# Four graph layers on one core: a chunk's first vector passes ordered behind layer 0's scaling, and half the node transfers of three groups begun on POOL's queue

## The chip, the cores and the metric

The kernel runs on one core of a Trainium2 chip. The metric is the device time of one execution in microseconds (us); lower is better. Each row of a table that comes from a trace is one execution; the medians are of several. Ratios are computed as the mean time of one kernel's runs over the mean of the other's of the same rounds, so they are not quite the ratios of the medians that are quoted. "Chunk" is 8 of the 128 graphs; "unit" is one of the 16 pieces into which layer 0's work is cut (0 to 2 of group 1, 3 and 4 of group 2, 5 and 6 of group 3, 7 and 8 of group 4, 9 to 15 of group 0).

## The reference

Four graph layers on 128 graphs of 64 nodes with 256 features, each followed by a residual and a layer norm. Only the parts that the argument touches:

```python
# layer 0: five groups of nodes, two normalised graph convolutions each
for g, idx in enumerate(GROUPS):            # 25, 9, 7, 6 and 6 of the first 25 nodes
    A = adj[:, idx][:, :, idx] + eye
    deg = A.sum(-1)
    norm_adj = deg**-0.5 * A * deg**-0.5
    h   = relu(norm_adj @ (x[:, idx] @ W1[g]) + b1[g])
    fused[:, idx] += w[g] * relu(norm_adj @ (h @ W2[g]) + b2[g])
x = layernorm(x + fused)
# layer 1: adj + eye, degree-normalised;   layer 2: a polynomial of adj / rowsum(adj)
# layer 3: five GRU steps on A = (adj != 0), the bulk of the matmuls
```

## The kernel before

TensorE's (PE's) instructions are issued in program order. The other engines' orders come from a scheduler at build time: it places an instruction where it expects its inputs to be there, and may move it well ahead of its place in the program. `tc.issue_after(ins)` adds an order behind `ins` on the same engine; it adds no wait.

The first passes over a chunk (`mid`) and the loads of layer 0:

```python
def mid(c):
    a64 = adjs.pop(c)                                    # the chunk's adjacency, loaded on SyncE's queue
    Ab = keep.tile([128, NP, 128], F32, name="Ab", bufs=1)
    nc.vector.tensor_mul(Ab..., a64..., pair...)         # first pass
    A01 = ...                                            # Ab != 0
    nc.vector.tensor_reduce(rsum, a64, AX.X, ALU.add)    # second reader of the load
    ...                                                  # rdeg, rinv, d1 (a power on POOL), dg, An
    nc.scalar.activation(poly, dg, AF.Identity, scale=cw[:, 2:3])
    yield                                                # [cut: transposes, products, layers 1 and 2]

def load0(i, after=None):
    qx = nc.gpsimd if i < 3 else nc.sync
    # [cut: tiles and the list of runs]
    for rows, t, b, f in runs:
        qa[t % len(qa)].dma_start(a[rows, t, :w], adj[b, f, 0:w])
    with tc.issue_after(after.ins) if after else nullcontext():
        for rows, t, b, f in runs:
            qx.dma_start(xg[rows, t, :], x[b, f, :])

def prep(i):                                             # on VectorE, with one power on POOL:
    # ae = a + eye; deg; d0 = deg**-0.5; ae *= d0; A0 = blocks of ae
    # PE transposes A0 into PSUM; then the "scaling of transposes":
    for v in scale:
        with tc.high_priority():
            evictions.append(nc.vector.tensor_mul(*v))   # AT

for i in range(-2, NU + 1):
    # [cut] add(i-1), aggregate(i+1), support(i), finish(i-1); then a stage of mid;
    # prep(i+2), hidden(i+1); at i == g0 (9): load_adj(0), load_adj(1)
```

## Time and profile before

| | before |
|---|---|
| device time, median of 3 | 2215.43 us (2214.81 to 2216.5) |
| span of the profiled execution | 2214.5 us |
| PE busy | 2180.2 us, 98% |
| PE idle | 34.3 us, of which 17.6 in one place at 106 to 125 us |
| first product of layer 3 | at 349.14 us |

Read it from PE: an engine that is busy 98% of the time leaves only its gaps to win, and what it does slowly; one gap is half of all gaps. The traced execution took 2216.3 us and is none of the three. The lines that show it are in the prediction below.

### The profile page before, as it was taken

How to read it: one execution, taken by the hardware profiler on the slowest of the kernel's cores; microseconds unless marked ns; L12 is line 12 of the kernel's file. 1: busy time of each engine (PE TensorE's matmuls, PEld its weight loads, DVE VectorE, ACT ScalarE, POOL GpSimd, SP SyncE). 2: the span in 40 equal slices, each digit the busy share in tenths (PEclk: the TensorE clock that was granted, in tenths of full speed). 3: DMA queues.
4: the chain of work that ended last, by engine and by line, in shares of the span. 5: the costliest groups of instructions: out<-in, count | busy, mean ns of one | idle time of the engine just before them, and what ended most of it. 6: DMA issues, size and time to landing. Idle time of an engine off the chain costs nothing.

```text
span 2214.5 us, 30166 instructions
## 1 busy us (share of the span) xinstructions
PE 2180.2 (98%) x11542; PEld 1911.4 (86%) x11542; DVE 1372.5 (62%) x3088; ACT 1003.1 (45%) x1853; POOL 571.0 (26%) x621
## 2 busy tenths in 40 slices
PE   9979999999999999999999999999999999999997
PEld 6657888888889889888889898888898898888886
DVE  3344666665766666666766676657666666566546
ACT  3233334445545454445454454455454544455453
POOL 3211122222222223223222222222222232232221
PEclk9989999999999999999999999999999999999999
DMA  5531210000100000000100010001000000000000
GB/s 166 178 109 55 58 46 4 1 3 1 41 1 4 1 20 22 3 1 7 35 1 3 1 41 1 3 1 41 1 1 1 20 10 1 1 10 11 1 1 20
DMA packets 54172, 51.12 MB, mean 23 GB/s; under 512 B 20878, under 2 KB 49036, under 8 KB 54028
## 3 DMA queue, kind: packets, MB, share of 16 engines
q1 hardware_dynamic: 49664, 43.96, 6.5%
q0 software_dynamic: 1936, 4.83, 0.8%
q8 instruction: 91, 1.49, 0.3%
q10 hardware_dynamic: 2428, 0.41, 0.1%
q14 instruction: 53, 0.43, 0.1%
HBM read 32.40 MB, written 16.78 MB: 22 GB/s over the span
## 4 chain that ended last, share of the span: by engine, by line
PE 94%; SPq 2%; DVE 1%; issue 1%; DMA 1%; ACT 0%; POOL 0%; POOLq 0%; DVEq 0%; ACTq 0%
PE parz L731 25%; PE pdrz L731 12%; PE pan L731 12%; PE pa L210 9%; PE pbrz L731 6%; PE pdn L731 6%; PE pT L772 4%; PE ps L442 4%; PE ph L426 3%; PE pbn L731 3%; PE pd L286 2%; PE pd L307 2%; SPq L362 1%; PE pa L411 1%; PE po L464 1%
## 5 line engine op out<-in xcount | busy, mean ns | idle before, releaser
L748 ACT COPY c<-parz 128x512 f32<-128x512 f32 x240 | 140.6, 586 | 322.4 <-PE parz L731 321.7
L731 PE MATMUL parz<-Th,WHH 128*128 128x256 f32 x960 | 286.0, 379 | 0.3 <-ACT c L748 0.3
L731 PE MATMUL parz<-Ta,V 128*128 128x256 f32 x960 | 285.8, 379 | 0.0
L711 POOL TENSOR_TENSOR Th<-hn 128x512 f32<-128x512 f32 x64 | 81.4, 1272 | 778.3 <-DVE hn L834 602.8
L831 ACT ACTIVATE NI<-NI,bih 128x512 f32<-128x512 f32 (+1 forms) x162 | 115.9, 715 | 206.0 <-DVE NI L826 205.8
L748 ACT COPY c<-pan 128x512 f32<-128x512 f32 x237 | 139.0, 586 | 150.1 <-PE pan L731 150.1
L731 PEld LDWEIGHTS parz<-Ta,V 128*128 128x128 f32 x960 | 182.5, 190 | 24.7
L731 PEld LDWEIGHTS parz<-Th,WHH 128*128 128x128 f32 x960 | 176.5, 191 | 21.1 <-ACT c L748 0.7
L803 ACT ACTIVATE RZ<-RZ,brz 128x512 f32<-128x512 f32 x160 | 116.0, 726 | 138.9 <-DVE RZ L760 138.9
L711 POOL TENSOR_TENSOR Ta<-agg 128x512 f32<-128x512 f32 x80 | 102.0, 1275 | 260.0 <-ACT agg L214 260.0
L760 DVE TENSOR_TENSOR RZ<-pdrz,c 128x512 f32<-128x512 f32 x80 | 55.0, 688 | 173.2 <-PE pdrz L731 173.2
L139 POOL TENSOR_TENSOR rs<-ve,mhalf 128x4 f32<-128x4 f32 (+3 forms) x67 | 68.9, 1029 | 298.3 <-DVE ve L137 234.4
L731 PE MATMUL pan<-Ta,V 128*128 128x256 f32 x474 | 141.3, 380 | 0.0
L731 PE MATMUL pan<-Th,WHH 128*128 128x256 f32 x474 | 141.1, 379 | 0.0
L754 DVE TENSOR_TENSOR NI<-pbn,c 128x512 f32<-128x512 f32 x79 | 54.6, 692 | 127.8 <-PE pbn L731 110.2
L210 PEld LDWEIGHTS pa<-A,h 128*128 128x128 f32 x1024 | 124.4, 192 | 3.3
L210 PE MATMUL pa<-A,h 128*128 128x128 f32 x1024 | 124.6, 275 | 0.0
L750 DVE TENSOR_TENSOR NI<-pdn,c 128x512 f32<-128x512 f32 x79 | 54.5, 689 | 112.7 <-ACT c L748 112.7
L832 DVE TENSOR_TENSOR RZ<-hn,NI 128x512 f32<-128x512 f32 (+1 forms) x129 | 87.8, 680 | 49.5 <-ACT NI L831 49.5
L834 DVE TENSOR_TENSOR hn<-RZ,NI 128x512 f32<-128x512 f32 (+1 forms) x161 | 109.8, 682 | 1.8
L833 DVE TENSOR_TENSOR RZ<-RZ 128x512 f32<-128x512 f32 (+1 forms) x161 | 109.5, 680 | 1.8
L442 PE MATMUL ps<-W,hg 128*125 128x256 f32 (+5 forms) x464 | 103.6, 380 | 0.3 <-ACT v L313 0.3
(220 smaller groups left out, 5077.0 us busy)
## 6 DMA issues: line engine op xcount, KB each, us to landing
out_dram<-xt SPq DMA_DIRECT2D x32, 256.0 KB
W<-in_w_dram SPq DMA_DIRECT2D x10, 512.0 KB
xt<-xb SPq DMA_DIRECT2D x32, 156.0 KB
xo<-in_x_dram SPq DMA_DIRECT2D x9, 512.0 KB
xb<-xo SPq DMA_DIRECT2D x9, 512.0 KB
xt<-xa SPq DMA_DIRECT2D x32, 100.0 KB
xg<-in_x_dram SPq DMA_DIRECT2D x25, 125.0 KB
xa<-xg SPq DMA_DIRECT2D x25, 125.0 KB
```

Source lines behind the costliest of these rows:

```text
L139: nc.gpsimd.tensor_tensor(rs[:r, :n], ve[:r, :n], mhalf[:r, :n], ALU.pow)
L210: nc.tensor.matmul(p[:, q * 128 : (q + 1) * 128], src[:, q, k * 128 : (k + 1) * 128], m[:, q, :], start=True, stop=True)
L442: nc.tensor.matmul(p[: u.rows[t], t - v, :], hg[:, e, u.off[t] : u.off[t] + u.rows[t]], W2[:, u.g, e, :], start=e == 0, stop=e == 3,)
L711: nc.gpsimd.tensor_sub(t[:, 0:2, :], a[:, :, H:], a[:, 0, :].rearrange("p (s n) -> p s n", s=2))
L731: nc.tensor.matmul(bank[:, g, :], w[:, q, i - 1, :], rhs, start=i in (1, 2, 5) and g == 0 and m == 0, stop=m == len(side) - 1, skip_group_ ...
L748: nc.scalar.copy(c, self.a)
L772: nc.tensor.transpose(p[:, q * 128 : (q + 1) * 128], src(q, k), ident)
L803: nc.scalar.activation(RZ[:, q, 0, :], RZ[:, q, 0, :], AF.Sigmoid, bias=b[0])
L831: nc.scalar.activation(n, n, AF.Tanh, bias=bih[:, 4 + j : 5 + j])
L832: e.tensor_sub(d, self.hT[:, j, f], n)
L833: e.tensor_mul(d, d, z)
L834: e.tensor_add(self.hn[:, j, f], d, n)
```

## The change

Its intent: the chunk's first passes shall not stand in front of layer 0's preparations, and SyncE's queue, which begins one transfer after another, shall be rid of part of its load.

```diff
-        nc.vector.tensor_mul(
-            Ab..., a64..., pair...)
+        with tc.issue_after(evictions[-1].ins):
+            nc.vector.tensor_mul(
+                Ab..., a64..., pair...)
         A01 = keep.tile([128, NP, 128], F32, name="A01", bufs=4)
         nc.vector.tensor_scalar(A01, Ab, 0.0, None, op0=ALU.not_equal)
-        nc.vector.tensor_reduce(rsum, a64, AX.X, ALU.add)
+        with tc.issue_after(evictions[-1].ins):
+            nc.vector.tensor_reduce(rsum, a64, AX.X, ALU.add)
@@ load0
-            qx = nc.gpsimd if i < 3 else nc.sync
+            qx = [nc.gpsimd] if i < 3 else [nc.sync, nc.gpsimd] if u.g > 1 else [nc.sync]
@@
-                    qx.dma_start(xg[rows, t, :], x[b, f, :])
+                    qx[t % len(qx)].dma_start(xg[rows, t, :], x[b, f, :])
```

(The operands of the first pass are shortened here.) "Part one" is the order, "part two" the queue.

More of the change, by code (lines that the diff above doesn't have):

```diff
@@ L225, in mid @@
         Ab = keep.tile([128, NP, 128], F32, name="Ab", bufs=1)
-        nc.vector.tensor_mul(
-            Ab.rearrange("p q (b m) -> p q b m", b=2),
-            a64[:, :, None, :].to_broadcast([128, NP, 2, N]),
-            pair[:, None, :, :].to_broadcast([128, NP, 2, N]),
-        )
+        with tc.issue_after(evictions[-1].ins):
+            nc.vector.tensor_mul(
+                Ab.rearrange("p q (b m) -> p q b m", b=2),
+                a64[:, :, None, :].to_broadcast([128, NP, 2, N]),
+                pair[:, None, :, :].to_broadcast([128, NP, 2, N]),
+            )
         A01 = keep.tile([128, NP, 128], F32, name="A01", bufs=4)
```

## The prediction

> **What bounds the kernel now.** I read first the page's busy shares and the chain that ended last, then the list of whom TensorE (PE) waited for, then the engines' timelines around the longest of those waits.
>
> ```profile
> PE 2180.2 (98%) x11542; PEld 1911.4 (86%) x11542; DVE 1372.5 (62%) x3088; ACT 1003.1 (45%) x1853; POOL 571.0 (26%) x621
> PE 94%; SPq 2%; DVE 1%; issue 1%; DMA 1%; ACT 0%; POOL 0%; POOLq 0%; DVEq 0%; ACTq 0%
> ```
>
> PE is busy 98% of the span and is 94% of the chain. The time can therefore only fall by what PE stands idle, or by what it does slowly; the span of 2214.5 less 2180.2 busy leaves 34.3 us. The chain has 2% on SyncE's queue (SPq) and 1% on a DMA: one place where PE is not the bound. The waits of PE say which:
>
> ```profile
> PE pT L397 <- DVE A L389: 15.1, 1, 15.1
> PE pT L860 <- DVE hn L834: 4.1, 3, 1.6
> PE ph L426 <- ACT ag L416: 2.5, 1, 2.5
> PE pf L560 <- ACT w L700: 1.9, 1, 1.9
> ```
>
> One wait of 15.1 us is almost half of the idle time, and the 2.5 us one follows directly after it. The timeline of VectorE (DVE) shows what DVE was doing (columns: start, duration, engine, line, operation; in brackets the idle time before it and what ended it):
>
> ```profile
> 93.63 0.16 DVE L121 TENSOR_TENSOR d0s<-deg,d0z 126x4 f32<-126x4 f32 x1
> 119.25 0.69 DVE L226 TENSOR_TENSOR Ab<-a,pair 128x512 f32<-128x512 f32 x1 [25.46 <-DMA a<-in_adj_dram]
> 119.86 0.15 DVE L125 SCALAR_TENSOR_TENSOR d0o<-deg,d0r 126x4 f32<-126x4 f32 x1
> 120.26 0.17 DVE L386 TENSOR_TENSOR ae<-ae,d0o 126x24 f32<-126x24 f32 x1
> 120.68 0.75 DVE L389 TENSOR_TENSOR A<-ae,block 126x252 f32<-126x252 f32 x2
> ```
>
> The reader is to see that chunk 0's first pass, Ab (line 226), stands in DVE's order in the middle of the preparation of layer 0's unit 7 (0 to 15, four units before the one where the program calls the chunk). It waits 25.5 us for the chunk's adjacency. The three steps behind it need only unit 7's own data, and PE needs their result. Why the adjacency is late is in SyncE's timeline: its load is issued behind eight node transfers.
>
> ```profile
> 104.39 7.57 SPq L362 DMA_DIRECT2D xg<-in_x_dram  x8
> 112.00 2.35 SPq L191 DMA_DIRECT2D a<-in_adj_dram  x2
> ```
>
> What PE lost is in its own timeline, with an undisturbed pair of the same shapes from two units later:
>
> ```profile
> 99.71 6.64 PE L442 MATMUL ps<-W,hg 128*126 128x256 f32 x30
> 121.48 1.10 PE L397 MATMUL pT<-ident,A 126*126 126x126 f32 x4 [15.13 <-DVE A L389]
> 125.07 5.31 PE L426 MATMUL ph<-ag,W 128*128 128x264 f32 x16 [2.48 <-ACT ag L416]
> 130.22 1.95 PE L464 MATMUL po<-AT,s 126*128 126x126 f32 x16
> ...
> 157.67 3.73 PE L426 MATMUL ph<-ag,W 128*128 128x264 f32 x16
> 161.24 1.95 PE L464 MATMUL po<-AT,s 126*128 126x126 f32 x16
> ```
>
> The same 16 matmuls take 5.31 us after the stall and 3.73 us later: the stall also costs clock. The table of stretches shows it (us, busy by engine, granted clock, DMA share, GB/s):
>
> ```profile
> 121.00:125.00 4.00, 1.10 (x4) 0.71 (x4) 3.10 (x19) 1.58 (x4) 1.39 (x1) 0.50 0.63 169
> 125.00:131.00 6.00, 5.93 (x24) 4.99 (x24) 3.95 (x18) 3.19 (x8) 2.43 (x2) 0.74 0.30 110
> 131.00:140.00 9.00, 9.00 (x55) 6.87 (x54) 5.78 (x33) 3.65 (x6) 2.24 (x3) 1.00 0.40 119
> ```
>
> **What the Trainium skill says.** (1) "TensorE: Matmul & The Clock Gate", the paragraph on engine queue depths: ACT and DVE are strict FIFO. The trace agrees: d0o needed a power that POOL had started at 93.93 us and that took 1.01 us, yet it ran at 119.86, right behind Ab. (2) Same page, Part 1 on the clock gate: an idle window of about 3.4 us drops the array to half clock, and about as long a busy stretch restores it. The trace agrees: 0.50 after the stall, 0.74, then 1.00. (3) "DMA: Bandwidth & Descriptors", "Issuing engines are not separate DMA queues": issuing from several engines saves only sequencer time. So the second part can buy issue time on SyncE, not bandwidth. No number of this trace tests it directly. (4) "SBUF — State Buffer", "SBUF: two separate sides": a DMA begun on POOL needs POOL to write descriptors, which some DVE operations lock out. In this trace POOL's node transfers land in 2.6 to 4.7 us beside a working DVE; I see no lockout.
>
> **Part one: Ab and the row sum behind the scaling of transposes.** The edge fixes an order on DVE and adds no wait. Chunk 0's first stage is called at unit index 10, when the last scaling of transposes traced is unit 11's, which ran at 188.68 us; Ab now comes behind it, some 69 us after its data arrived (119.25). So Ab waits for nothing, and unit 7's preparation runs on: power until 94.94, d0o, the 0.17 us scaling and two products of together 0.75 us, done at about 96.5 by the durations above. PE reaches those transposes at 106.34, so about 10 us of slack. The 15.1 us wait goes.
> The 2.5 us wait goes with it: ScalarE's copy ag stood in order behind the chunk's poly (line 248, run at 123.42 after 26.03 us of idling for DVE's dg), which also moves back.
> The gain, from the chain in order of time: PE's products end at 106.34 and the po group begins at 130.38, 24.04 us. Undisturbed, four transposes (157.40 to 157.84, 0.44 us) and sixteen matmuls (3.56 us) take 4.00. The gain is 24.04 - 4.00 = **20.0 us**: 15.1 + 2.5 of waiting and the rest slow clock.
> What it moves: Ab 0.6, A01 0.3, rsum 0.3, An 0.6, dg 0.6 and eight small ones of 0.08 each, some 3 us of DVE, from the stall to behind 188.68 on the old clock. Unit 12's preparation there ended at 199.04 and PE came for it at 206.54: 7.5 us of slack takes the 3 us. Chunk 0's own transposes come at 213.85. For chunk 1 the pass goes behind unit 14's scaling (253.43), with its transposes at 267.0; DVE is busy 13.5 of 20 us there, so it fits with less room. Later chunks had their passes long after layer 0, so the edge binds nothing; row sums of chunks 2 and 3 that ran early move to the end of layer 0, where DVE is fuller. I allow 0.5 us for both.
>
> **Part two: half the node transfers of groups 2 to 4 on POOL.** Units 3, 4, 5 and 7 give 4 of 8 issues each, units 6 and 8 (three tiles) 2 of 6: 20 issues. SyncE sheds 20 x 0.736 us = 14.7 us of issuing; POOL gains 20 x 0.62 = 12.4 us by the median of its ten node issues. Once part one is in, the adjacency has some 70 us to spare and PE waits for no other load, so 14.7 us of earlier issue is worth nothing directly. The cost: POOL is on the preparation's path through the power of 1.01 us. Four issues in front of a power hold it 2.5 us. Most preparations end 5 to 9 us before PE wants them, but unit 1's ends at 16.6 for 18.7, and unit 4's at 54.2 for 54.8. Units 3 to 5 also have unused buffers, so their transfers may be begun early, about 11 to 18 us, where the DMA engines were busiest (0.88 in the first 20 us) and where DVE waited 3.65 us for unit 1's adjacency. I allow 1 us on average for new waits here.
>
> **Sum.** 2215.43 - 20.0 + 0.5 + 1.0 = 2196.9, say 2197 us, 0.8% less.
>
> **The rivals.** (a) A wait takes the place of the old one: behind DVE's Ab stand the passes over other nodes (xo), loads of 512 KB that took 10.4 us once, and with PE 20 us earlier DVE may come to one too soon. For: the SyncE queue is in the chain. Against: DVE's waits show no xo load, and SyncE gets 14.7 us lighter. It would leave 5 to 10 us of the gain away: 2202 to 2207. (b) POOL becomes the trouble: powers of units 1 and 4 held by issues, or early loads slowed. For: slacks of 2.1 and 0.6 us. Against: POOL is busy only 26%. It would cost 3 to 8 us, with a cold clock where a stall passes some microseconds: 2198 to 2204. (c) Part two alone is what helps, the adjacency then coming 15 us earlier at about 104 us, and part one nothing more. It would give the same time within the stall's 20 us, so it can't be told by the total. (d) Something in the long third layer shifts: PE has 98% there and no wait of note, so nothing I see.
>
> **Range and chances.** All 34.3 us of idle gone would be 2181, and 2% is 44 us (below 2171): faster by 2% is out of reach of this change. Slower by 2% would need new stalls of 64 us against the gain. The range goes from the gain with nothing given back and 2 us of luck (2193) to rival (a) at its worst (2207).
>
> **What would show it right or wrong.** Right: the 15.1 and 2.5 us waits are gone from PE's list, Ab stands behind unit 11's scaling with no DMA wait, the granted clock is 1.00 from 20 to 335 us, PE's busy time falls by some 2 us, and layer 3 starts 18 to 20 us sooner. Part one is wrong if another DVE wait stops PE between 95 and 330 us; part two if a wait of PE before 60 us goes back to a POOL power or a load. The prediction fails if the gain is under 8 us, or over 22.

## The result, and the profile after

The changed kernel takes 2197.85 us (median of 4, 2197.42 to 2199.79) beside 2215.97 us of the kernel before: ratio 0.9919, 95% interval 0.9902 to 0.9937. That is 18 us or 0.8% less. The prediction was 2197 us.

The lines of the page and of PE's waits that answer to those of before:

```profile
PE 2178.3 (99%) x11542; PEld 1908.3 (87%) x11542; DVE 1372.5 (62%) x3088; ACT 1003.1 (46%) x1853; POOL 583.1 (27%) x641
```

```profile
PE pT L862 <- DVE hn L836: 4.3, 3, 1.8
PE pf L562 <- ACT w L702: 1.9, 1, 1.9
PE pw L536 <- DVE zero L533: 1.5, 1, 1.5
```

The waits of 15.1 and 2.5 us are gone and none has come in their place. PE's busy time is 1.9 us less for the same 11542 matmuls. The timeline of VectorE (DVE) around unit 7's preparation, and where Ab is now (start, duration, then engine, line, operation, output and input; idle time before in brackets; "..." marks lines left out):

```profile
94.75 0.16 DVE L121 TENSOR_TENSOR d0s<-deg,d0z 126x4 f32<-126x4 f32 x1
96.09 0.16 DVE L125 SCALAR_TENSOR_TENSOR d0o<-deg,d0r 126x4 f32<-126x4 f32 x1 [1.19 <-POOL d0r L123]
...
96.51 0.75 DVE L391 TENSOR_TENSOR A<-ae,block 126x252 f32<-126x252 f32 x2
...
107.93 0.68 DVE L403 TENSOR_TENSOR AT<-pT,d0o 126x504 f32<-126x504 f32 x1 [7.78 <-PE pT L399]
...
169.74 0.68 DVE L403 TENSOR_TENSOR AT<-pT,d0o 125x500 f32<-125x500 f32 x1 [8.08 <-PE pT L399]
...
175.23 0.66 DVE L227 TENSOR_TENSOR Ab<-a,pair 128x512 f32<-128x512 f32 x1
175.88 0.41 DVE L236 TENSOR_REDUCE rsum<-a 128x4 f32<-128x256 f32 x1
```

Between the steps d0s and d0o there is now only the power on POOL (1.19 us of idle time in place of 25.5 us). The products A are done at 97.3 us and PE takes them at 107.29. Ab runs at 175 us behind unit 11's scaling, with no wait for its load. The timeline of PE, and the granted clock in the stretch that held the stall (columns as in the prediction):

```profile
107.29 0.60 PE L399 MATMUL pT<-ident,A 126*126 126x126 f32 x4
107.72 3.73 PE L428 MATMUL ph<-ag,W 128*128 128x264 f32 x16
111.29 1.95 PE L466 MATMUL po<-AT,s 126*128 126x126 f32 x16
...
330.28 0.59 PE L733 MATMUL parz<-hT,WHH 128*128 128x256 f32 x2
```

```profile
100.00:121.00 21.00, 21.00 (x115) 17.44 (x115) 7.47 (x38) 7.11 (x13) 2.24 (x3) 1.00 0.47 149
```

The sixteen matmuls take 3.73 us in place of 5.31, and PE is busy for all of these 21 us, with a granted clock of 1.00. SyncE begins the adjacency at 93.42 us in place of 112.00, 18.6 us sooner:

```profile
82.50 10.87 SPq L364 DMA_DIRECT2D xg<-in_x_dram  x8
93.42 2.35 SPq L191 DMA_DIRECT2D a<-in_adj_dram  x2
```

**Where the time went, in three stretches.** The profiled executions are split at the first transposes of unit 0 and at the first product of layer 3.

| stretch | before | after | difference |
|---|---|---|---|
| start to first transposes | 8.58 | 9.65 | +1.07 |
| first transposes to layer 3 | 340.56 | 320.63 | -19.93 |
| layer 3 to the end | 1865.36 | 1865.92 | +0.56 |
| span | 2214.5 | 2196.2 | -18.3 |

The gain is all in the middle stretch, and it is nearly the 20.04 us worked out. For the first stretch the cause is not shown. PE's warm-up products begin at 1.49 us in both and take 7.26 us before, 8.32 us after; three traced executions of the changed kernel took 8.32, 7.06 and 7.79 us for them, so one program varies by as much. Yet over all traces the first transposes lie at 9.07 to 9.76 us in the nine with both edges of part one and at 8.55 to 8.86 us in the four without. In two of the nine PE waited there behind a load (0.66 us in after_again, for a preparation whose adjacency came late; 0.96 us in all_pool, for the identity). Whether the change has a part in it stays open. The third stretch hides a full microsecond, which the experiments trace: from ScalarE's last scaling to the end it is 3.82 us before and 4.83 us after.

### The profile page after: what moved, and what is told of

Its sections match the earlier page's. It is cut to its first block, busy times and chain, and to the rows that moved or that the text cites.

```text
span 2196.2 us, 30203 instructions
## 1 busy us (share of the span) xinstructions
PE 2178.3 (99%) x11542; PEld 1908.3 (87%) x11542; DVE 1372.5 (62%) x3088; ACT 1003.1 (46%) x1853; POOL 583.1 (27%) x641
## 3 DMA queue, kind: packets, MB, share of 16 engines
q8 instruction: 91, 1.49, 0.3%
## 4 chain that ended last, share of the span: by engine, by line
PE 96%; DVE 2%; issue 1%; POOL 1%; ACT 0%; DMA 0%; POOLq 0%; ACTq 0%; DVEq 0%
PE parz L733 25%; PE pdrz L733 12%; PE pan L733 12%; PE pa L210 9%; PE pbrz L733 6%; PE pdn L733 6%; PE ps L444 4%; PE ph L428 4%; PE pT L774 4%; PE pbn L733 3%; PE pd L288 3%; PE pd L309 2%; PE pa L413 1%; PE po L466 1%; PE pp L278 1%
```

## The experiments

All outputs are right. In the table, "middle" is the stretch from the first transposes to layer 3 and "end" the time from the start of ScalarE's last scaling to the end, both from the profiled execution; "POOL" is the number of transfers begun on POOL's queue in all.

| run | median us | ratio to before | middle | end | POOL |
|---|---|---|---|---|---|
| before | 2213.48 to 2214.83 | 1 | 340.56 | 3.82 | 31 |
| after_again | 2197.91 | 0.9926 (0.9914 to 0.9938) | 320.66 | 4.84 | 51 |
| order_only | 2196.83 | 0.9921 (0.9909 to 0.9933) | 320.59 | 3.81 | 31 |
| pool_only | 2210.94 | 0.9985 (0.9971 to 0.9999) | 336.59 | 4.85 | 51 |
| ab_edge_only | 2220.26 | 1.0025 (1.001 to 1.0039) | 342.02 | 3.84 | 31 |
| early_adj | 2211.38 | 0.9984 (0.9971 to 0.9998) | 332.06 | 3.79 | 31 |
| all_pool | 2208.68 | 0.9975 (0.9961 to 0.9988) | 328.67 | 6.82 | 75 |
| order_stores4 | 2197.59 | 0.9927 (0.9915 to 0.994) | 323.23 | 4.01 | 31 |
| order_stores2 | 2196.76 | 0.9923 (0.991 to 0.9937) | 320.60 | 3.71 | 31 |
| after_fewer | 2197.06 | 0.9923 (0.9911 to 0.9936) | 320.10 | 3.81 | 39 |
| order_again | 2197.97 | 0.9925 (0.9912 to 0.9939) | 320.59 | 3.86 | 31 |
| after_third | 2198.32 | 0.993 (0.9917 to 0.9942) | 320.59 | 4.80 | 51 |

The profiled execution of order_stores4 is the slowest of its five (2199.57); its middle is 2.6 us longer than that of its sister order_stores2, with a granted clock of 0.95 from 300 to 333 us. Executions as slow come in other builds too (2199.46 of after_again, 2198.34 of order_only, 2200.05 and 2199.75 of after_third); what sets them off was not followed.

The builds that keep a stall vary more: the kernel before took 2210.51 to 2219.22 us, part one alone 2196.42 to 2198.34. A "middle" with a stall in it is therefore good to a few microseconds only. The traced execution of the kernel before is some 2 us above its later medians, that of pool_only is the slowest of its four, those of ab_edge_only and early_adj the fastest of theirs.

### after_again: the changed kernel as the measure

No edit.

> The changed kernel unaltered, as the measure for the others on the same chip. Both theories: 2197 to 2200 us, ratio to the kernel before 0.991 to 0.993. The start of its first transposes should differ between executions by up to about 1 us (9.65 us in the profile of the changed kernel, 8.58 before), if that difference is the phase of the clock gate and not the change.

The time is as expected: 2197.91 us. The first transposes came at 9.21 us, with the same program as the one of 9.65. That does not show the clock as the reason: here the warm-up products were done sooner (7.06 us in place of 8.32), and PE then waited 0.66 us for a preparation.

### order_only: part one alone

```diff
-            qx = [nc.gpsimd] if i < 3 else [nc.sync, nc.gpsimd] if u.g > 1 else [nc.sync]
+            qx = [nc.gpsimd] if i < 3 else [nc.sync]
```

> Part one alone (Ab and row sum behind the scaling of transposes), all node transfers of groups 2 to 4 on SyncE again. My theory, that the order on VectorE is the whole gain: within 1.5 us of the changed kernel, 2196 to 2199 us; the chunk's adjacency is still issued late, at about 112 us, and nobody waits for it; no TensorE wait over 2 us before 330 us. Rival, that the transfers on POOL are needed for the gain (SyncE's queue would become the bound once the stall is gone): over 2203 us, with a wait of VectorE or TensorE for a load.

Measured: 2196.83 us, the middle stretch 320.59 us. The whole gain is there without part two. SyncE's timeline and VectorE's show why the late load doesn't matter:

```profile
112.44 2.20 SPq L191 DMA_DIRECT2D a<-in_adj_dram  x2
```

```profile
174.64 0.66 DVE L227 TENSOR_TENSOR Ab<-a,pair 128x512 f32<-128x512 f32 x1
```

The load is as late as in the kernel before (112.00), and its first reader stands 62 us behind its issue. The rival, that SyncE would become the bound, falls.

### pool_only: part two alone

The two lines of `load0` on the kernel before, without the edges on Ab and the row sum.

> Part two alone. Rival (c) of the prediction, that an adjacency issued 15 us earlier ends the stall by itself: 2197 to 2201 us. My theory, that the order is what counts: in this build Ab stands in VectorE's order one unit earlier still, in the preparation of unit 6, whose transposes TensorE wants at about 89 us; the load is issued at about 93 and lands at about 100, so VectorE waits from 78 to 100 and TensorE 10 to 15 us, and the time is 2208 to 2216 us: the 15 us won on SyncE are eaten by the earlier place.

Measured: 2210.94 us, in the range of the order theory and far from the rival's. The load was indeed begun 22.6 us sooner (89.40 us), but the scheduler had moved Ab forward with it, from unit 7's preparation into unit 6's. VectorE's waits and PE's:

```profile
DVE Ab L226 <- DMA a<-in_adj_dram: 18.0, 1, 18.0
```

```profile
PE pT L397 <- DVE A L389: 9.6, 2, 8.8
PE ph L426 <- ACT ag L416: 2.8, 2, 2.4
```

VectorE waits 18.0 us in place of 25.5, PE 12.4 in place of 17.6, and the middle stretch gains 4.0 us of 20 (by the medians the kernel gains 2.5 us). An earlier load under a scheduler that follows it is worth much less than its 22.6 us.

### ab_edge_only: half of part one

```diff
         with tc.issue_after(evictions[-1].ins):
             nc.vector.tensor_mul(Ab..., a64..., pair...)
-        with tc.issue_after(evictions[-1].ins):
-            nc.vector.tensor_reduce(rsum, a64, AX.X, ALU.add)
+        nc.vector.tensor_reduce(rsum, a64, AX.X, ALU.add)
```

(without part two.)

> Part one halved: only Ab is held back, the row sum of the same load is free, and no transfers on POOL. My theory, that any pass on the late load stops VectorE: the row sum stands in unit 7's preparation where Ab stood, waits some 25 us for the adjacency, TensorE waits 13 to 16 us, and the time is 2212 to 2217 us. Rival, that Ab alone made the wait and the row sum came only after it: 2197 to 2200 us.

Measured: 2220.26 us, 0.25% slower than the kernel before and above my range. The row sum took Ab's place, as expected. But PE was stopped by another way than I wrote:

```profile
115.82 0.42 DVE L235 TENSOR_REDUCE rsum<-a 128x4 f32<-128x256 f32 x1 [21.79 <-DMA a<-in_adj_dram]
```

```profile
118.55 0.72 ACT L249 ACTIVATE poly<-dg,cw 128x512 f32<-128x512 f32 x1 [23.54 <-DVE dg L245]
```

```profile
PE ps L443 <- ACT hg L431: 18.9, 1, 18.9
```

ScalarE's poly, three steps behind the row sum, stood in ScalarE's order between two of layer 0's activations (hg). ScalarE kept its order too: it idled 23.5 us in front of poly with hg behind it, and PE waited 18.9 us for hg. So holding back one reader freed nothing here while another reader of the same load was left. The edge on the row sum alone was not run.

### early_adj: neither part, only an earlier call of the load

```diff
-            elif i == g0:
-                for c in (0, 1):
-                    load_adj(c)
             elif i == 4:
+                for c in (0, 1):
+                    load_adj(c)
```

> Neither part of the change; only the call that loads the adjacency of chunks 0 and 1 stands five units earlier in the program. My theory, that the stall is the time from when TensorE wants a preparation to when the load in front of it lands, whatever the load's own place: VectorE's order follows the load forward, Ab stands in unit 6's preparation (wanted by TensorE at about 88 us), the load is issued at about 83 and lands at 90 to 92, so TensorE waits 3 to 8 us plus some 2 us for ScalarE's copy and slow clock: 2202 to 2209 us, between the kernel before and the changed one. Rival, that an earlier load simply mends it: 2195 to 2199 us. Rival, that the load's place is without effect because the order adapts fully: 2212 to 2217 us.

Measured: the profiled execution 2207.63 us, the other three 2211.15 to 2211.88; median 2211.38, 2 us above my range, so the sizing missed. The load was begun at 80.39 us and Ab's wait came as worked out, but a second wait was not in my account (the trace is of the fastest execution, so it need not hold all of the median's loss):

```profile
85.84 0.69 DVE L226 TENSOR_TENSOR Ab<-a,pair 128x512 f32<-128x512 f32 x1 [10.89 <-DMA a<-in_adj_dram]
118.09 0.42 DVE L234 TENSOR_REDUCE rsum<-a 128x4 f32<-128x256 f32 x1 [12.48 <-DMA a<-in_adj_dram]
```

The second is chunk 2's row sum, which the scheduler moved into unit 7's preparation once its buffer was free sooner; PE waited 3.3 us there for the scaling of transposes. Together with pool_only this settles that moving the load is no cure: the reader moves with it.

### all_pool: part two at more than twice the dose

```diff
-            qx = [nc.gpsimd] if i < 3 else [nc.sync, nc.gpsimd] if u.g > 1 else [nc.sync]
+            qx = [nc.gpsimd] if i < 3 or u.g > 1 else [nc.sync]
```

> The changed kernel with all node transfers of groups 2 to 4 on POOL, twice the dose of part two (44 issues in place of 20). My theory, that POOL has room: the stretch from the first transposes of layer 0 to layer 3's first products stays at 320.3 to 321.5 us (20 issues: 320.6), and the time within 1.5 us of the changed kernel. Rival (b) of the prediction, that issues hold POOL's powers: waits of TensorE for a preparation before 60 us, 2199 to 2204 us. The end after ScalarE's last scaling was 3.8 us in the builds without part two and 4.8 in those with it: if transfers on POOL cause that, it grows to about 6; if the position of the last store among the eight semaphores that the queues use in turn causes it (the same here as in the changed kernel), it stays at 4.8.

Measured: 2208.68 us, above even the range that the rival gave (2199 to 2204). My theory that POOL has room is wrong at this dose, and rival (b) of the prediction holds. In POOL's timeline fourteen transfers stand in front of the power that unit 2's preparation needs, and the first of them waits for POOL's own earlier transfers to land; VectorE and PE wait behind:

```profile
24.76 8.07 POOL L364 DMA_DIRECT2D xg<-in_x_dram  x14 [3.52 <-DMA xg<-in_x_dram]
32.70 1.25 POOL L123 TENSOR_TENSOR d0r<-d0s,mhalf 126x1 f32<-126x1 f32 x2
```

```profile
33.46 0.16 DVE L125 SCALAR_TENSOR_TENSOR d0o<-deg,d0r 126x1 f32<-126x1 f32 x1 [9.33 <-POOL d0r L123]
```

PE waits 3.9 us for that preparation, and its matmuls after it run slowly (8.72 us where 7.03 is usual). That is 5.6 of the 8.0 us by which the middle stretch is longer. Some 1.7 us more are slow matmuls before it, behind the wait for the identity (3.03 and 7.72 us where 2.05 and 7.03 are usual), and 0.5 us a later wait for a preparation. With 20 transfers the same power was not held: in the changed kernel it ran at 21.86 us, and VectorE waited 0.4 us for it. The end grew too, from 4.8 to 6.8 us, which speaks for POOL's transfers as its cause and against the position of a semaphore.

### order_stores4 and order_stores2: does the last semaphore's position set the end?

Part one alone, with this besides:

```diff
-                for h in range(2):
-                    nc.sync.dma_start(ov[self.c][:, 2 * h : 2 * h + 2], self.xt[:, 2 * h : 2 * h + 2])
+                m = 1 if self.c in (0, 1) else 2        # order_stores2: (0,)
+                for h in range(0, NP, m):
+                    nc.sync.dma_start(ov[self.c][:, h : h + m], self.xt[:, h : h + m])
```

> Part one alone, and chunks 0 and 1 stored in four pieces each in place of two: four stores more in the middle of the program, so that the last store uses the semaphore it has in the changed kernel (index 1 of 8, not 5). No transfers of groups 2 to 4 on POOL. If the position of the last semaphore in the closing waits costs the end: 4.8 us after ScalarE's last scaling, and some 1.0 us more than part one alone, 2197 to 2199 us. If transfers on POOL cost it: 3.8 us and the time of part one alone, 2196 to 2198 us.

> Part one alone, and chunk 0 stored in four pieces: two stores more, the last store then uses index 7 of 8. If each closing wait behind the last one to be met costs a fixed time (1.0 us over the four places between index 1 and 5, so about 0.25 each): 3.3 us at the end, and the fastest version, 2195.5 to 2197.5 us. If not: 3.8 us.

Measured: 4.01 and 3.71 us at the end, where a position effect asked for 4.8 and 3.3. That theory falls; what is left of it is 0.3 us at most. What differs among the builds is the closing drain on POOL's queue. The lines of the program's closing instructions, from order_only, the changed kernel, all_pool and, taken from the run below, after_fewer (count; shortest, middle and longest in ns; first and last start):

```profile
L1045 POOLq DRAIN  x3: 51/97/3367, 2189.8 to 2194.3; - x3
```

```profile
L1045 POOLq DRAIN  x3: 51/93/4997, 2190.4 to 2195.9; - x3
```

```profile
L1045 POOLq DRAIN  x3: 51/93/6957, 2199.2 to 2206.7; - x3
```

```profile
L1045 POOLq DRAIN  x3: 51/102/4018, 2190.3 to 2194.9; - x3
```

The longest of the three drains is 3.367, 4.997 and 6.957 us with 31, 51 and 75 transfers begun on POOL: (6.957 - 3.367) / 44 = 0.0816 us each, and 0.0816 x 20 = 1.63, as measured between 31 and 51. In every other trace it is the same: 3.365 to 3.367 us with 31 transfers, 4.997 or 4.998 with 51. In order_only the drain ends at about 2193.2 us and SyncE, which waits for the last store, goes on at 2193.7: there the drain is hidden. In the changed kernel it ends at 2195.4, 0.8 us behind SyncE's 2194.6.

### after_fewer, order_again, after_third: the drain tested

after_fewer is the changed kernel with twelve other transfers moved from POOL to SyncE:

```diff
-  nc.gpsimd.dma_start(ih[:, q], wihT...)         # x3, wls[l] x5, WHH and w21 x4
+  nc.sync.dma_start(ih[:, q], wihT...)
```

> The changed kernel with twelve other transfers (layer 3's weights: three ih, five wl, four of WHH) taken from POOL's queue to SyncE's, so that POOL begins 39 in all in place of 51. The closing drain on POOL took 3.37 us with 31 transfers, 5.00 with 51 and 6.96 with 75: 0.0816 us each and 0.84 fixed. Theory: with 39 it takes 4.02 us, about as long as the last store needs to land, and the end after ScalarE's last scaling falls from 4.84 to 3.8 to 4.0 us; time about that of part one alone, 2196 to 2198 us, if SyncE has room for the twelve. Rival, that part two's own transfers cost the end and not the count: the end stays at 4.8 us.

> Part one alone once more, as the fastest version so far, beside the run above and the changed kernel below: 2196 to 2198 us, about 1 us under the changed kernel, with 3.8 us at the end.

> The changed kernel once more on the same chip: 2197 to 2200 us, 4.8 us at the end.

Measured: a drain of 4.018 us where 4.02 was worked out, an end of 3.81 us, and 2197.06 us. Part two is still in that kernel, so it is the count that costs and not the size: those twelve are of 192 and 256 KB, the node transfers of 126 KB or less. order_again and after_third show 3.86 and 4.80 us at the end. Over both calls, part one alone is 1.1 and 1.2 us faster than the changed kernel by the means of the same rounds (2196.99 to 2198.09, 2197.54 to 2198.72). That is half a thousandth; the intervals of the ratios overlap, and the trace is the firmer evidence. Part one alone is likely the better version, by about a microsecond.

## Why the prediction was right

**The bound and the gap: right.** The idle time of PE was the only thing to win, and its largest piece was an in-order engine stopped by one early instruction. order_only shows the cause: with the load as late as before and only the order changed, the wait is gone. The signs that the prediction named came too: the granted clock is 1.00 from 20 to 335 us, and layer 3 starts 18.9 us sooner.

**The size of part one: right for the traced execution, less on average.** Worked out 20.0 us; in the traces the middle stretch fell by 19.93 to 19.97. But both sides of that use the same trace of the kernel before, the one of 2216.3 us. By the means of the same rounds part one alone gained 17.3 us (order_only) and 16.9 us (order_again), and the intervals of the ratios allow 13.5 to 20 us. What one stall costs was measured well, what it costs on average less so. Counting the slow clock after the stall was needed: waits alone were 17.6 us.

**What part one moves: right in kind, less in size.** I allowed 0.5 us for 3 us of VectorE's work given back; by the middle stretch some 0.1 us was given back.

**Part two worth nothing directly: right.** The adjacency was begun 18.6 us sooner, more than the 14.7 us worked out, and order_only is not slower without it.

**The allowance of 1 us for part two: the number right, the place wrong.** I put it on POOL's powers and on early loads. With 20 transfers neither cost PE anything. The microsecond was lost at the other end of the program, in POOL's closing drain, which no step of the prediction had. Another microsecond of the profiled span was lost at the start, for a reason that stays open. So it is partly luck that 2197 was met within 1 us: the 1.5 us allowed for losses and the losses found (1.0 at the end, 1.1 at the start of the traced execution) lie in different places, and the later calls put the gain of the whole change at 16.2 and 15.7 us by the means, where 18.5 was forecast.

**The rivals.** (a), a wait on the other nodes' loads, did not come. (b) is real but needs more than this dose: all_pool shows it, at some 6 of the 8.0 us by which its middle stretch is longer (328.67 less 320.63). (c), that part two alone would do it, fell: 4.0 us of 20. The prediction had said that the total could not tell (c) apart; that was so, and it took the two halves run alone to tell. (d) saw nothing in layer 3, and nothing was there but the end.

## What to carry to other kernels

When an engine that runs in order stands idle on a load, look at who stands behind the waiting instruction: moving that instruction back in the order gained 17 us here and cost 0.1, while hastening the load gained 2.5 us, because the scheduler moved the reader forward with it. Hold back every reader of the load, or the next one takes its place, and what depends on it can stop another engine. Before transfers are moved to another engine's queue, ask what that engine computes behind them and what the queue costs at the end; here the transfers were worth nothing and cost a microsecond.

## What the Trainium skill lacked or had wrong

- "VectorE: DVE Perf Modes", "The DRAIN you can't avoid", describes the runtime's own DRAIN instructions as about 12 ns each on all five engines. Whether the closing ones here are of that kind is not known; the twelve of the changed kernel take 7 to 4997 ns. One closing DRAIN on POOL's queue took 3.367, 4.018, 4.997 and 6.957 us with 31, 39, 51 and 75 transfers begun there: 0.0816 us each and 0.84 us fixed, on the program's end once it outlasts the last store. No page gives a closing cost per transfer begun on POOL.
- "DMA: Bandwidth & Descriptors", "Issuing engines are not separate DMA queues", says that issuing from several engines only saves the sequencer's issue time. The saving is confirmed (SyncE's adjacency load 18.6 us sooner in the changed kernel), but the passage leaves out that POOL's issues stand in order before POOL's computing: in all_pool fourteen of them took 8.07 us, and VectorE waited 9.33 us for the power behind them (0.41 us for the same power in the changed kernel).
- "TensorE: Matmul & The Clock Gate", Part 1, says that the moment of warming up varies from run to run. This agrees, so nothing is to be mended there: the twelve warm-up matmuls took 8.32, 7.06 and 7.79 us in three executions of the changed kernel.
